# Attention and mixture-of-experts layers on one core: fused clips, rows transposed in place, ScalarE's order pinned, pieces of the schedule moved

## The chip, the cores and the metric

The kernel runs on one core of a Trainium2 chip. The metric is the device time of one execution in microseconds (us). A core has five engines that work side by side, each with a queue of its own: TensorE (PE in the profile; PEld is its loading of weights), VectorE (DVE), ScalarE (ACT), GpSimd (POOL) and SyncE (SP, which here only issues DMAs). All arithmetic is in f32.

## The reference, cut to what matters

Four layers run one after another over x of 8 sequences x 512 tokens x 256 features: attention a, experts, attention b, experts again with the same weights. Each layer adds to x a function of the normalised x.

```python
def attn_a(x):                       # 16 heads of 64
    q, k, v = split(x @ w_qkv)
    sim = (q * 64**-0.5) @ k.T + slopes * -abs(i - j)
    return softmax(where(j > i, -max, sim)) @ v @ w_out + b_out

def attn_b(x):                       # 8 heads of 128
    q, k = rope(x @ w_aq), rope(x @ w_ak)
    s = q @ k.T / 128 - 1e30 * (i < j)
    return softmax(s) @ (x @ w_av) @ w_ao

def ffn(x):                          # 8 experts, the best 2 of each token
    h = x * rsqrt(mean(x * x) + eps) * norm_w
    vals, idx = top_k(h @ gate_w.T + gate_b, 2)
    wts = softmax(vals)
    t1 = einsum('td,efd->tef', h, mlp1_w) + mlp1_b
    glu = minimum(t1[..., ::2], 7.0)
    lin = clip(t1[..., 1::2], -7.0, 7.0)
    act = glu * sigmoid(1.702 * glu) * (lin + 1.0)
    y = einsum('tei,edi->ted', act, mlp2_w) + mlp2_b
    return x + sum(y[idx] * wts)

x = x + attn_a(layernorm(x)); x = x + ffn(layernorm(x))
x = x + attn_b(layernorm(x)); x = x + ffn(layernorm(x))
```

## The kernel before

Tokens lie in tiles of 128 partitions, four to a sequence (`NT`). Only PE's order is that of the program; on the other engines the framework's scheduler orders instructions by its own estimate of when each is ready, except those that `keep_in_program_order` pins among each other.

**Attention.** `layer` steps through 8 sequences and 8 head groups. A step (`Attention.step`) puts on PE the scores of the current group, the transposes of the previous one (`turn`), the projections of the next and the weighted average of the previous. Scores get bias and row minimum on DVE (L387), exp on ACT (L397), and are divided by their sum on DVE and POOL (L412). Between these, `extra` runs pieces hung on a step: loading and normalising the next sequence, the output projection of the last one, and the first parts of the experts of the previous sequence.

**Choosing experts.** For each sequence `Experts.norm`, `apply`, `turn_norm`, `gates`, `choose` and `count` normalise x, store the rows h in DRAM, find each token's two experts and weights and count them. `choose` turns the gap of the two best logits into weights with an exp on ACT and three small DVE operations. For a group of sequences (six, then two: `GROUPS`), `sorting` then works out in pieces (`slots`, `pair`, `invert`, `tokens`) which token goes into which row of which block.

**Expert blocks.** `Experts.run` walks 55 + 23 blocks of 128 rows, each of one expert, as a software pipeline on PE: in turn n it issues `gather` for block n+4 (an indirect DMA on POOL, L867), `turn_act` for n-4 (transposes L927, ACT copy aT L929), `turn_rows` for n (transposes gtp L880, ACT copy hT L882), `first` for n-1 (matmuls hp L902, then on DVE and ACT the bias L912, clip L913, sigmoid L914, clip L916, products L917 and L918), and `second` for n-4 (matmuls y L937, bias L947, scatter of the rows to DRAM L948 on POOL). Then it runs the pieces hung on turn n, in `aside`.

Buffers limit how far this runs ahead: eight gathered rows (tag "qk", two tiles of `ROWS` = 4), four "S" tiles for the activations u, eight "kb" tiles that hold hT, aT and much else, and two "V" tiles for y.

**Pieces between blocks.** `flush` hangs on the first turns of an expert pass what attention left for the last sequence: the transposes and average of its last step, two pieces of output projection, then norm, apply, turn_norm, gates, choose and count; and after them the second group's sorting, three turns apart. From turn `done` (60), when the first group's rows are all written, the first pass fetches sequence 0 back for attention b and adds its expert rows; the second pass goes through six sequences by halves, fetching x, collecting rows (`collect`, L982) and adding (`add`, L1018), two turns apart, then stores the result (L1141). After the blocks the last two sequences are fetched, collected, added and stored.

## Time and profile before

| what | us |
|---|---|
| runs shown: median of 3 | 2336.51 |
| runs shown: lowest, highest | 2333.77, 2343.92 |
| profiled execution, its time | 2302.66 |
| its span, first to last instruction | 2300.8 |
| PE busy in the span | 2229.6 |

The stretches of the span are: attention a from the start to about 925 us, expert blocks to about 1196, attention b to about 2007, expert blocks to about 2276, then the last sums. In the profile's rows a name such as hp_f stands for the buffer written or read, `<-` parts output from inputs, `x` counts instructions. The bracket at the end of a row of the timeline is the engine's idle time before it and what ended it. A wait for several signals is put down to the one that came last. Idle time of an engine that is not the limit costs nothing. PE's instructions overlap, so two matmul rows can cover the same time.

### The profile page before, as it was taken

What the parts mean: (1) busy time and instruction counts of PE and PEld (TensorE: products, weight loads), DVE (VectorE), ACT (ScalarE), POOL (GpSimd) and SP (SyncE); (2) the same over time, 40 slices, a digit from 0 to 9 for tenths busy, and PEclk for the clock granted to TensorE, in tenths of its full rate; (3) what the DMA queues carried; (4) which work ended last, traced back from release to release, by engine and by line L of the source; (5) the groups of instructions that cost most, each with busy time, mean ns of one, the idle gap of its engine ahead of it and who ended that gap; (6) DMA issues with size and microseconds to landing.
All of it is one profiled execution on the core that took longest, in us unless ns stands there. A gap on an engine that the chain in (4) does not pass through costs nothing.

```text
span 2300.8 us, 34673 instructions
## 1 busy us (share of the span) xinstructions
PE 2229.6 (97%) x10657; PEld 1452.9 (63%) x10657; DVE 1635.5 (71%) x4926; ACT 977.9 (43%) x2828; POOL 989.9 (43%) x1374
## 2 busy tenths in 40 slices
PE   8999999999999999899999999999999999999994
PEld 5666666666666666556556666666666666665662
DVE  5566666666666777687877677776867678778787
ACT  4555555555555555323234343443433433433331
POOL 5443434343433343556644333343433434445662
PEclk9999999999999999999999999999999999999997
DMA  7100000000000001222310011010101000022247
GB/s 241 38 28 1 28 1 29 1 28 1 28 1 28 6 28 70 99 79 88 103 52 15 10 37 33 15 46 5 42 10 37 14 33 28 19 78 81 88 156 231
DMA packets 80005, 112.54 MB, mean 49 GB/s; under 512 B 10288, under 2 KB 64720, under 8 KB 79824
## 3 DMA queue, kind: packets, MB, share of 16 engines
q1 hardware_dynamic: 63760, 68.37, 9.0%
q0 software_dynamic: 14976, 40.91, 5.7%
q8 instruction: 89, 1.46, 0.3%
q10 hardware_dynamic: 1088, 1.05, 0.2%
q14 instruction: 92, 0.75, 0.1%
HBM read 68.86 MB, written 41.44 MB: 48 GB/s over the span
## 4 chain that ended last, share of the span: by engine, by line
PE 88%; DVE 7%; issue 2%; POOL 2%; ACT 1%; DMA 1%; DVEq 0%; ACTq 0%; POOLq 0%; SPq 0%
PE pp_a L317 9%; PE pp_b L317 9%; PE hp_f L902 9%; PE op_a L454 6%; PE sp_a L375 6%; PE tp_a L427 6%; PE sp_b L375 6%; PE op_b L454 5%; PE yp_b L472 5%; PE yp_a L472 5%; PE vp_a L298 5%; PE vp_b L298 5%; PE y_f L937 5%; PE tp_b L427 3%; PE atp_f L927 1%
## 5 line engine op out<-in xcount | busy, mean ns | idle before, releaser
L397 ACT ACTIVATE S_a<-S_a,nm_a 128x512 f32<-128x512 f32 (+3 forms) x512 | 280.3, 549 | 306.6 <-DVE nm_a L387 306.5
L330 POOL TENSOR_TENSOR qk_b<-qk_b,rot_b 128x512 f32<-128x512 f32 x128 | 162.8, 1272 | 457.0 <-DVE qk_b L329 446.8
L902 PE MATMUL hp_f<-we,hT_f 128*128 x624 | 294.4, 594 | 0.8 <-ACT hT_f L882 0.8
L356 POOL TENSOR_SCALAR ali_a<-alibi 128x512 f32<-128x512 f32 x128 | 79.4, 620 | 451.0 <-DVE nm_a L387 442.5
L397 ACT ACTIVATE S_b<-S_b,nm_b 128x512 f32<-128x512 f32 (+3 forms) x256 | 142.8, 558 | 235.3 <-DVE nm_b L387 233.8
L387 DVE CUSTOM_DVE_ANT_0 S_a<-sp_a,ali_a 128x512 f32<-128x512 f32 (+3 forms) x512 | 215.9, 486 | 30.7 <-PE sp_a L375 30.5
L412 POOL TENSOR_SCALAR S_a<-S_a,sum_a 128x384 f32<-128x384 f32 (+2 forms) x384 | 205.5, 551 | 34.7 <-DVE sum_a L408 26.2
L948 POOL DMA_INDIRECT y_f<-y_f,row_f x156 | 155.5, 997 | 131.6 <-DVE y_f L947 100.4
L867 POOL DMA_INDIRECT g_f<-h_all_f,token_f x156 | 152.1, 975 | 99.9 <-PE gtp_f L880 58.0
L914 ACT ACTIVATE u_f<-u_f 128x256 f32<-128x256 f32 x156 | 65.1, 417 | 305.0 <-DVE u_f L913 304.8
L937 PEld LDWEIGHTS y_f<-we,aT_f 128*128 128x128 f32 x624 | 117.2, 191 | 110.7 <-issue 53.3
L937 PE MATMUL y_f<-we,aT_f 128*128 x624 | 164.8, 387 | 21.6 <-ACT aT_f L929 21.6
L387 DVE CUSTOM_DVE_ANT_0 S_b<-sp_b,mask 128x512 f32<-128x512 f32 (+3 forms) x256 | 119.1, 484 | 90.5 <-PE sp_b L375 90.5
L375 PE MATMUL sp_b<-qk_b 128*128 128x512 f32 (+3 forms) x512 | 171.9, 438 | 5.0 <-POOL qk_b L330 5.0
L427 PE MATMUL tp_a<-ident,S_a 128*128 128x128 f32 x1280 | 165.3, 276 | 1.1 <-DVE O_a L462 0.6
L427 PEld LDWEIGHTS tp_a<-ident,S_a 128*128 128x128 f32 x1280 | 141.1, 141 | 31.9 <-issue 22.8
L454 PE MATMUL op_a<-PT_a,V_a 128*64 128x384 f32 (+3 forms) x1024 | 154.2, 439 | 3.3 <-ACT PT_a L437 2.2
L912 DVE TENSOR_TENSOR u_f<-hp_f,be 128x512 f32<-128x512 f32 x156 | 107.8, 691 | 68.8 <-PE hp_f L902 61.0
L375 PE MATMUL sp_a<-qk_a 64*128 64x512 f32 (+3 forms) x1024 | 155.5, 443 | 0.9 <-DVE qk_a L334 0.9
L902 PEld LDWEIGHTS hp_f<-we,hT_f 128*128 128x128 f32 x624 | 106.8, 191 | 76.0 <-issue 74.8
L437 ACT COPY PT_a<-tp_a 128x512 f32<-128x512 f32 (+1 forms) x320 | 138.6, 495 | 29.4 <-PE tp_a L427 29.4
L454 PE MATMUL op_b<-PT_b,V_b 128*128 128x512 f32 (+3 forms) x512 | 148.6, 433 | 0.0
(184 smaller groups left out, 4505.6 us busy)
## 6 DMA issues: line engine op xcount, KB each, us to landing
h_all_f<-hn_f SPq DMA_DIRECT2D x64, 128.0 KB, 1.7
xm_f<-x_mid_f SPq DMA_DIRECT2D x16, 512.0 KB, 4.1
yg_f<-y_f SPq DMA_DIRECT2D x64, 128.0 KB, 2.2
yg_f<-y_f SPq DMA_DIRECT2D x28, 256.0 KB, 4.0
x<-x_in_dram SPq DMA_DIRECT2D x8, 512.0 KB, 4.1
we<-w_dram SPq DMA_DIRECT2D x8, 512.0 KB, 7.1
x_mid_f<-x SPq DMA_DIRECT2D x8, 512.0 KB, 2.9
x_mid_f<-xm_f SPq DMA_DIRECT2D x8, 512.0 KB, 3.0
```

The lines of the kernel that those rows point to most:

```text
L298: nc.tensor.matmul(vp[:, k, :], lhsT=self.xT[b][:, c, t * P : (t + 1) * P], rhs=wv[:, c, q * 2 * P : (q + 1) * 2 * P], start=(c == 0), sto ...
L317: nc.tensor.matmul(pp, lhsT=w[:, c, g * P : (g + 1) * P], rhs=self.xT[b][:, c, :], start=(c == 0), stop=(c == NC - 1),)
L330: nc.gpsimd.tensor_tensor(qk[:, j, :], qk[:, j, :], rot, ALU.add)
L375: nc.tensor.matmul(sp[i][:, at[it] : at[it] + w], lhsT=qk[r, 0, it * P : (it + 1) * P], rhs=qk[r, 1, 0:w], start=True, stop=True,)
L387: nc.vector.tensor_tensor_reduce(out=s, in0=sp[i][:, at[it] : at[it] + w], in1=add[i][:, T - w : T], scale=scale, scalar=float(np.finfo(np ...
L397: nc.scalar.activation(s, s, AF.Exp, bias=nm[:, it : it + 1], scale=-1.0, accum_out=sums[:, it : it + 1],)
L412: eng.tensor_scalar(s, s, sums[:, it : it + 1], 1.0, ALU.mult, ALU.mult)
L427: nc.tensor.transpose(tp[:, o : o + P], S[:, S_OFF[it] + jt * P : S_OFF[it] + (jt + 1) * P], ident,)
L454: nc.tensor.matmul(op[i * cols : (i + 1) * cols, jt * P : T], lhsT=v[:, jt, c0 : c0 + cols], rhs=PT[i][:, P_OFF[jt] : P_OFF[jt] + T - jt * P],
L472: nc.tensor.matmul(yp[:, 0:D], lhsT=o[:, c, t * P : (t + 1) * P], rhs=wo[:, half * HALF + c, :], start=(c == 0), stop=(c == HALF - 1),)
L902: nc.tensor.matmul(hp, lhsT=h[:, c * P : (c + 1) * P], rhs=we_sb[:, bass.DynSlice(wat + c * 2 * FI, 2 * FI)], start=(c == 0), stop=(c == N ...
L937: nc.tensor.matmul(yp, lhsT=aT[:, c * P : (c + 1) * P], rhs=we_sb[:, bass.DynSlice(wat + NC * 2 * FI + c * D, D)], start=(c == 0), stop=(c ...
```

## The change

- **Clips.** The minimum of the gate half, L913, goes. The sigmoid reads the unclipped value; the product with the other half clips it on the way, and the product with the sigmoid clips that at sigmoid(1.702 x 7). Output g has a place of its own.
- **In place.** hT is written over the gathered rows, aT over the first half of t.
- **ScalarE's order.** The copies hT and aT and the sigmoid are pinned.
- **Start.** The first sequence comes in four transfers on two queues, and PE does 24 transposes of the identity that nothing reads.
- **Choose.** In the last sequence of a pass both weights are sigmoids of the gap and of its negative.
- **Pieces.** `flush` hangs its pieces on other turns, the sorting four turns apart. In the second pass x comes back in pairs into attention's weight buffers at turns 24 to 42; halves are collected 1.5 turns apart into two tags by turns, added four turns later, and stored by one DMA. The last two sequences have no fetch of their own, and their stores alternate between SP's and ACT's queue.

```diff
+S_LIMIT = float(1.0 / (1.0 + np.exp(-ALPHA * LIMIT)))
...
-    X = {0: load_x(x_in[0], "x0")}
+    X = {0: xpool.tile([P, NT, D], F32, tag="x", name="x0")}
+    for t in range(NT):
+        (nc.sync, nc.scalar)[t % 2].dma_start(
+            out=X[0][:, t, :], in_=x_in[0][t * P : (t + 1) * P, :]
+        )
...
     make_identity(nc, ident)
+    idle = ps.tile([P, P], F32, tag="ps", bufs=8, name="idle")
+    for _ in range(24):
+        nc.tensor.transpose(idle, ident, ident)
...
+            if among_blocks:
+                for k in range(2):
+                    nc.scalar.activation(
+                        r["w"][k][:, here], gap, AF.Sigmoid, scale=(1.0, -1.0)[k]
+                    )
+            else:
...
-            h = work.tile([P, D], F32, tag="kb", bufs=8, name=f"hT_{key}")
-            nc.scalar.copy(h, tp)
+            h = g
+            made = nc.scalar.copy(h, tp)
+            tc.keep_in_program_order(made)
...
-            t, g, a = u[:, 0 : 2 * FI], u[:, 2 * FI : 3 * FI], u[:, 3 * FI : 4 * FI]
-            s = u[:, 4 * FI : 5 * FI]
+            t, s = u[:, 0 : 2 * FI], u[:, 2 * FI : 3 * FI]
+            g, a = u[:, 3 * FI : 4 * FI], u[:, 4 * FI : 5 * FI]
+            lin = t[:, FI : 2 * FI]
             nc.vector.tensor_tensor(t, hp, be_sb[:, bass.DynSlice(bat, 2 * FI)], ALU.add)
-            nc.vector.tensor_scalar(g, t[:, 0:FI], LIMIT, 1.0, ALU.min, ALU.mult)
-            nc.scalar.activation(s, g, AF.Sigmoid, scale=ALPHA)
-            lin = t[:, FI : 2 * FI]
+            made = nc.scalar.activation(s, t[:, 0:FI], AF.Sigmoid, scale=ALPHA)
+            tc.keep_in_program_order(made)
             nc.vector.tensor_scalar(lin, lin, 1.0 - LIMIT, 1.0 + LIMIT, ALU.max, ALU.min)
-            nc.vector.tensor_tensor(g, g, lin, ALU.mult)
-            nc.vector.tensor_tensor(a, g, s, ALU.mult)
-            self.act[i, j] = a, wat, bat
+            nc.vector.scalar_tensor_tensor(g, t[:, 0:FI], LIMIT, lin, ALU.min, ALU.mult)
+            nc.vector.scalar_tensor_tensor(a, s, S_LIMIT, g, ALU.min, ALU.mult)
+            self.act[i, j] = a, t[:, 0:FI], wat, bat
...
-            aT = work.tile([P, FI], F32, tag="kb", bufs=8, name=f"aT_{key}")
-            nc.scalar.copy(aT, tp)
+            made = nc.scalar.copy(aT, tp)
+            tc.keep_in_program_order(made)
...
+        def fetch_pair(self, b, tag):
+            pair = wpool.tile([P, 2, NT, D], F32, tag=tag, name=f"xm_{self.kind}_{b}")
+            for k in range(2):
+                X[b + k] = pair[:, k]
+                nc.sync.dma_start(out=pair[:, k], in_=by_tokens(self.x_mid[b + k]))
...
-        turns = (1, 2, 3, 4, 4, 5, 7, 8, 9, 11)
+        turns = (-3, 0, 1, 1, 1, 3, 6, 8, 10, 12)
...
-            aside[14 + 3 * n] = [piece]
+            aside[16 + 4 * n] = [piece]
...
-    n = done
-    for b in range(*GROUPS[0]):
-        aside.setdefault(n, []).append(lambda b=b: exp_b.fetch(b))
-        for tt in ((0, 1), (2, 3)):
-            aside.setdefault(n, []).append(
-                lambda b=b, tt=tt: exp_b.collect(b, tt, "PT", both_queues)
-            )
-            aside.setdefault(n + 3, []).append(lambda b=b, tt=tt: finish(b, tt))
-            n += 2
+    for k, tag in enumerate(("wq", "wk", "wv", "wo")):
+        aside.setdefault(24 + 6 * k, []).append(lambda k=k, tag=tag: exp_b.fetch_pair(2 * k, tag))
+    halves = [(b, tt) for b in range(*GROUPS[0]) for tt in ((0, 1), (2, 3))]
+    for k, (b, tt) in enumerate(halves):
+        n = done + 3 * k // 2
+        tag = ("xT", "PT")[k % 2]
+        aside.setdefault(n, []).append(
+            lambda b=b, tt=tt, tag=tag: exp_b.collect(b, tt, tag, both_queues)
+        )
+        aside.setdefault(n + 4, []).append(lambda b=b, tt=tt: finish(b, tt, nc.sync))
...
-    for b in range(*GROUPS[1]):
-        exp_b.fetch(b)
-        for tt in ((0, 1), (2, 3)):
-            exp_b.collect(b, tt, "S", (nc.sync, nc.scalar))
-    for b in range(*GROUPS[1]):
-        for tt in ((0, 1), (2, 3)):
-            finish(b, tt)
+    last = [(b, tt) for b in range(*GROUPS[1]) for tt in ((0, 1), (2, 3))]
+    for b, tt in last:
+        exp_b.collect(b, tt, "S", (nc.sync, nc.scalar))
+    for k, (b, tt) in enumerate(last):
+        finish(b, tt, (nc.sync, nc.scalar)[k % 2])
```

More of the change, by code (lines that the diff above doesn't have):

```diff
@@ L631, in gates, with choose @@
             self.h[b] = lgT
-        def choose(self, b):
+        def choose(self, b, among_blocks=False):
             kind = self.kind
@@ L670, in choose @@
             nc.vector.tensor_tensor(gap, top[0], top[1], ALU.subtract)
-            fall = t2("fall")
-            nc.scalar.activation(fall, gap, AF.Exp, scale=-1.0)
-            nc.vector.tensor_scalar_add(gap, fall, 1.0)
-            nc.vector.reciprocal(r["w"][0][:, here], gap)
-            nc.vector.tensor_tensor(r["w"][1][:, here], r["w"][0][:, here], fall, ALU.mult)
+            if among_blocks:
[4 more added lines that the diff above has]
+            else:
+                fall = t2("fall")
+                nc.scalar.activation(fall, gap, AF.Exp, scale=-1.0)
+                nc.vector.tensor_scalar_add(gap, fall, 1.0)
+                nc.vector.reciprocal(r["w"][0][:, here], gap)
+                nc.vector.tensor_tensor(r["w"][1][:, here], r["w"][0][:, here], fall, ALU.mult)
             self.both[b] = t3("both")
@@ L909, in first @@
             u = work.tile([P, PACKED], F32, tag="S", bufs=4, name=f"u_{key}")
-            t, g, a = u[:, 0 : 2 * FI], u[:, 2 * FI : 3 * FI], u[:, 3 * FI : 4 * FI]
-            s = u[:, 4 * FI : 5 * FI]
+            t, s = u[:, 0 : 2 * FI], u[:, 2 * FI : 3 * FI]
+            g, a = u[:, 3 * FI : 4 * FI], u[:, 4 * FI : 5 * FI]
+            lin = t[:, FI : 2 * FI]
             nc.vector.tensor_tensor(t, hp, be_sb[:, bass.DynSlice(bat, 2 * FI)], ALU.add)
-            nc.vector.tensor_scalar(g, t[:, 0:FI], LIMIT, 1.0, ALU.min, ALU.mult)
-            nc.scalar.activation(s, g, AF.Sigmoid, scale=ALPHA)
-            lin = t[:, FI : 2 * FI]
+            made = nc.scalar.activation(s, t[:, 0:FI], AF.Sigmoid, scale=ALPHA)
+            tc.keep_in_program_order(made)
             nc.vector.tensor_scalar(lin, lin, 1.0 - LIMIT, 1.0 + LIMIT, ALU.max, ALU.min)
-            nc.vector.tensor_tensor(g, g, lin, ALU.mult)
-            nc.vector.tensor_tensor(a, g, s, ALU.mult)
-            self.act[i, j] = a, wat, bat
+            nc.vector.scalar_tensor_tensor(g, t[:, 0:FI], LIMIT, lin, ALU.min, ALU.mult)
+            nc.vector.scalar_tensor_tensor(a, s, S_LIMIT, g, ALU.min, ALU.mult)
+            self.act[i, j] = a, t[:, 0:FI], wat, bat
         def turn_act(self, i, j):
             key = f"{self.kind}_{i}_{j}"
-            a, wat, bat = self.act.pop((i, j))
+            a, aT, wat, bat = self.act.pop((i, j))
             tp = ps.tile([P, FI], F32, tag="ps", bufs=8, name=f"atp_{key}")
@@ L998, in collect @@
             m = (b - GROUPS[i][0]) * NT + tiles[0]
-            bufs = {"S": 4, "PT": 2, "tmp": 3}[tag]
+            bufs = {"S": 4, "xT": 2, "PT": 2, "tmp": 3}[tag]
             got = work.tile(
@@ L1063, in layer @@
             put(b + 1, 4, 1, lambda b=b: exp.gates(b))
-            put(b + 1, 5, 1, lambda b=b: exp.choose(b))
+            put(b + 1, 5, 1, lambda b=b: exp.choose(b, b + 1 == NB))
             put(b + 1, 6, 1, lambda b=b: exp.count(b))
@@ L1117, in layers @@
     aside = flush(layer(att_a, exp_a, more), exp_a)
-    aside[6] = [weights_b]
+    aside.setdefault(6, []).append(weights_b)
     aside[done] = [lambda: exp_a.fetch(0)]
@@ L1136, in layers, with finish @@
     aside = flush(layer(att_b, exp_b, more), exp_b)
-    def finish(b, tiles):
+    def finish(b, tiles, engine):
         exp_b.add(b, tiles)
-        for t in tiles:
-            nc.sync.dma_start(out=by_tokens(out[b])[:, t, :], in_=X[b][:, t, :])
-    n = done
-    for b in range(*GROUPS[0]):
-        aside.setdefault(n, []).append(lambda b=b: exp_b.fetch(b))
-        for tt in ((0, 1), (2, 3)):
-            aside.setdefault(n, []).append(
-                lambda b=b, tt=tt: exp_b.collect(b, tt, "PT", both_queues)
-            )
-            aside.setdefault(n + 3, []).append(lambda b=b, tt=tt: finish(b, tt))
-            n += 2
+        engine.dma_start(
+            out=by_tokens(out[b])[:, tiles[0] : tiles[-1] + 1, :],
+            in_=X[b][:, tiles[0] : tiles[-1] + 1, :],
+        )
[7 more added lines that the diff above has]
+            lambda b=b, tt=tt, tag=tag: exp_b.collect(b, tt, tag, both_queues)
+        )
+        aside.setdefault(n + 4, []).append(lambda b=b, tt=tt: finish(b, tt, nc.sync))
     end = sum(BLOCKS) + 4
     exp_b.run(aside)
-    for m in range(end, n + 3):
+    for m in range(end, n + 5):
         for piece in aside.get(m, ()):
             piece()
-    for b in range(*GROUPS[1]):
-        exp_b.fetch(b)
-        for tt in ((0, 1), (2, 3)):
-            exp_b.collect(b, tt, "S", (nc.sync, nc.scalar))
-    for b in range(*GROUPS[1]):
-        for tt in ((0, 1), (2, 3)):
-            finish(b, tt)
+    last = [(b, tt) for b in range(*GROUPS[1]) for tt in ((0, 1), (2, 3))]
[3 more added lines that the diff above has]
+        finish(b, tt, (nc.sync, nc.scalar)[k % 2])
 def _tables():
```

## The prediction

> **What bounds the kernel now.** First the page: busy shares, then the span in 40 slices.
>
> ```profile
> PE 2229.6 (97%) x10657; PEld 1452.9 (63%) x10657; DVE 1635.5 (71%) x4926; ACT 977.9 (43%) x2828; POOL 989.9 (43%) x1374
> PE   8999999999999999899999999999999999999994
> ```
>
> TensorE is the bound; no edit removes a needed matmul, so all there is to win is the 71.2 us (2300.8 - 2229.6) in which it idles, and the stretches where it ran slowly. Busy time by stretch (stretch, length, PE, PEld, DVE, ACT, POOL, clock, DMA) places them:
>
> ```profile
> 0.00:58.00 58.00, 47.89 (x233) 29.38 (x233) 29.64 (x115) 28.09 (x85) 33.95 (x68) 1.00 0.70 239
> 900.00:1000.00 100.00, 91.30 (x463) 58.64 (x460) 74.48 (x258) 38.10 (x106) 48.79 (x60) 1.00 0.33 111
> 1000.00:1100.00 100.00, 100.00 (x406) 63.13 (x405) 81.54 (x215) 31.90 (x101) 64.04 (x66) 1.00 0.27 86
> 2275.00:2301.00 26.00, 0.65 (x4) 0.22 (x2) 13.79 (x31) 0.00 (x0) 1.99 (x2) 0.55 0.79 262
> ```
>
> Steady expert blocks run at 100%, one per 3.02 us. Idle are the start (10.1), the opening of each expert pass, its close, and the tail (25.4). The waits (total, times, longest) name the releaser:
>
> ```profile
> PE y_f L937 <- ACT aT_f L929: 21.6, 25, 2.4
> PE xtp_a L255 <- DVE xn_a L242: 8.6, 1, 8.6
> PE tp_b L427 <- POOL S_b L412: 2.5, 1, 2.5
> ```
>
> ACT is named for 21.6 us, but in the timeline it was itself held by DVE:
>
> ```profile
> 956.65 0.28 DVE L913 TENSOR_SCALAR u_f<-u_f 128x256 f32<-128x256 f32 x1
> 956.96 0.42 ACT L914 ACTIVATE u_f<-u_f 128x256 f32<-128x256 f32 x1 [5.65 <-DVE u_f L913]
> 957.28 0.35 ACT L929 COPY aT_f<-atp_f 128x256 f32<-128x256 f32 x1
> 957.69 1.13 PE L937 MATMUL y_f<-we,aT_f 128*128 x4 [2.45 <-ACT aT_f L929]
> 970.90 1.28 ACT L914 ACT_TABLE_LOAD   x1
> 972.92 1.13 PE L937 MATMUL y_f<-we,aT_f 128*128 x4 [1.19 <-ACT aT_f L929]
> ```
>
> The copy aT needs only PE's transposes, but stands in ACT's queue behind a later block's sigmoid, whose input waits for a burst of DVE work. The chain that ended last gives both ends:
>
> ```profile
> 0.73 4.22 DMA x<-x_in_dram
> 8.65 1.77 PE xtp_a L255 x7
> 11.18 5.41 PE pp_a L317 x8
> 23.52 1.72 PE pp_a L317 x4
> 2276.83 6.01 DMA y_f<-y_f,row_f
> 2285.95 5.70 DMA yg_f<-y_f
> ```
>
> Eight pp_a matmuls took 5.41 us where four later take 1.72: 3.44 at full clock.
>
> **The sum**, stage by stage, in the profiled execution's own time.
>
> **Start.** x0's statistics start at 4.97 when 512 KB has landed and end at 6.74. In four transfers the first three tiles' statistics (about 0.45 each) lie under the landing. 128 KB transfers elsewhere land in 1.7 to 2.2 us; here all four share the engines with wq, so I put the last at 4.7 (3.9 to 5.5), the end at 5.3: **1.4** saved (0.6 to 2.2). wq and wk are issued one DMA (0.44) later and land at about 7.9 and 10.5, needed at about 9.2 and 11.0. The two issues on ACT's queue come before its first 1.28 us table load, otherwise half the gain goes. The 24 transposes cost PE only idle time: at the slow 0.22 us each, 5.3 us from the identity's end at 1.47, so until 6.8, and xn arrives at about 7.1. Here row and rule differ. By the row half speed lasted 6.05 us, 8.65 to 14.70, so the warm clock would come at about 7.5. The Trainium skill (TensorE: Matmul & The Clock Gate, Part 1) wants one busy window of about 3.4 us, on a grid that runs free of the kernel: an estimate from it is clock up between 4.9 and 8.3. Row: pp_a falls from 5.41 to 3.44 and the transposes by 0.5, **2.5** saved. Rule at its late end: 0.5 less. The page's granted clock shows 1.00 here and doesn't decide it. I take the row; bounds 0 to 2.5. Start: **3.9** (0.6 to 4.7).
>
> **The block's own work.** DVE drops L913 (0.28; 0.21 net of overlap). The two fused products keep the tensor products' price: a fused one with a pointer scalar costs 480 ns (L1018) against 425 (L918), but with an immediate 0.19 both (L667, L663, 128x32); at worst 0.11 per block. L917 no longer overwrites what the sigmoid reads, a wait of 0.25 to 0.34 where DVE is behind. So 0.21 per block where PE covers it (worth nothing, 3.02 stays), about 0.45 where DVE is the limit. hT over g and aT over t remove no instruction. They hold buffers longer: u until L937, which precedes the next user's matmul on PE anyway; g's rows until hp instead of gtp, so every fourth gather waits about 4.7 us longer (y 0.86, the transposes 0.44, two hp 3.44). Scatters and POOL norms stand behind it. It still issues 10 us before its transposes, and gather plus landing is 1.0 + 2.8: hidden, 6 us to spare. The pinned ACT order (aT, hT, sigmoid) is the order the steady trace shows already: 0.
>
> **Opening of pass one.** L937's waits are 2.45 (norm applied), 1.19 (choose), 0.35 + 0.77 + 1.46 (slots, pairs). Choosing by sigmoid removes the last sequence's two table loads. By the row, 1.28 each with PE waiting 1.19; by the skill (ScalarE: Activation LUTs, What ACT_TABLE_LOAD costs) about 2.66 a switch, so 5.3 per pass. No second half is seen after the load: the sigmoid starts at 972.20, 1.30 after 970.90. I take 1.0. Norm to apply is now two short blocks (3.9) instead of one of 3.02, so DVE stands less behind POOL's rsqrt chain (1.86 there): 2.45 to 1.5, bounds 0 to 3. Sorting four blocks apart instead of three, with 0.21 freed in each: 2.58 to 1.1. Sum **3.4** (0 to 6). The moved last turn and average carry 20 transposes and their ACT/DVE copies; S_a is ready by 926.6, so 0. On SP, apply's four row stores and its x_mid store go two turns earlier; only weights_b stands behind them, needed 60 blocks later.
>
> **Close of pass one.** DVE-bound blocks of 4.06, 3.76, 4.10 and 3.89 us instead of 3.02, and one wait of 1.83. Four blocks at 0.45 and 1.2 off the wait (two sigmoids no longer stand behind L913, which took 0.80 and 0.86 there): **3.0**. Around 1192 to 1200 the clock fell to half after sparse work (about 3.1 lost); a third of that back: **1.0**. Bounds 1 to 7.5.
>
> **Opening of pass two.** The same 3.4, and half of a clock dip at 2042 to 2046 (1.7): 0.8. Against it: the last turn now stands ahead of every block, but S_b L412 sits behind eight gathers in POOL's queue until 2013.3. Gathers 0 and 1's transposes and hp(0), 2.5 us that filled this hole, come after: PE waits about 5.4 instead of 2.5. Net **1.7** (-3 to 9; the top if POOL serves S_b first).
>
> **Close of pass two and tail.** Twelve half-sequence sums (4 adds of 0.44) now come every 1.5 blocks: 1.17 us of DVE per block, not 0.88. With the rest of the block at 2.05 to 2.3 that is 3.2 to 3.45 against 3.02. Over 17 blocks 3.4 to 7.3, of which the pipeline absorbed 1.7 before; I put the stall at 2.5 and 0.5 in the drain. Before, 3.6 in blocks and 1.8 in the drain: **2.4**. The eight x fetches go earlier on SP (0.37 each, ahead of the collects; 4 MB in all, at blocks 24 to 42, when SP has nothing else), and the last out writes leave the tail (one DMA of 256 KB for two of 128; the final four alternate with ACT's queue, where nothing stands behind them), so the last scatter, 6.01 in traffic of 290 GB/s, lands in 3.5 (typical 2.5): **2.5**. From 2282.8 the before needs 17.9 us: about 4 MB at 330 GB/s, with the last reads held on SP to 2287.9 behind a fetch. After: first half at 4.0, four times 1.88 of adds, then 3.5 from last add to end as before: 15. **2.9**. Together **7.8** (2 to 13).
>
> Sum: 3.9 + 3.4 + 4.0 + 1.7 + 7.8 = **20.8 us**. The profiled execution took 2302.66 (span 2300.8 and 1.86 around it), so about 2282. The runs shown have a median of 2336.51, 33.85 above it, for which the profile gives no cause; I take the same difference off: **2315.7**.
>
> **Rivals.** (a) The waits only move: DVE's bursts are as long, and pinned ACT holds aT behind the sigmoid as before. For it: the 2.45 wait is just that order, unchanged. Openings give 1.0 each from table loads less 2.5, closes 2, start 3.9, tail 5.4: 10.8 saved, **2325.7**. (b) Everything recovers: both clock dips gone, S_b first on POOL, no stall at 1.5 blocks: start 4.7, 6 + 6, 6, 11: 33.7, **2302.8**. Against it: DVE's 3.2 per block. (c) Slower: gathers held until hp become late, PE waits at gtp. Price: x us for each of 39 groups of four rows. It cancels the gain at 0.53, and from 0.84 the kernel is over 0.5% slower; at 1.0, **2354.7**. Against it: POOL is busy 64 of 100 us and the 6 us to spare.
>
> **Numbers.** Main case 0.50, (a) 0.26, (b) 0.16, (c) 0.08. About 0.5% (11.7 us) is what this measurement can tell from nothing. Main and (b) are faster, (a) straddles 2324.8 evenly: faster 0.79, same 0.13, slower 0.08. The range runs from just under (b), 2300, to 2331, where (a) with its runs' spread of some 5 us ends; outside lie (c) and the edges.
>
> **What would show it.** pp_a's first eight at 3.5 us and sp_a starting near 13.6; one ACT_TABLE_LOAD per pass; L937's waits near 10 in total; tp_b's wait 5 if POOL keeps its order; DVE over 95% in the last 17 blocks; last scatter landing under 4 us and 15 us after it. It is wrong if PE waits at gtp_f on g_f, if half clock returns before xtp_a, or if L937's waits stay near 20.

## The result and the profile after

| | us |
|---|---|
| before, 8 runs: median (lowest to highest) | 2342.24 (2333.77 to 2344.70) |
| changed, 8 runs: median (lowest to highest) | 2325.02 (2317.98 to 2332.04) |
| changed / before | 0.9939, 95% interval 0.9918 to 0.9959 |
| profiled execution of the changed kernel, its span | 2324.46, 2322.7 |

The change makes the kernel about 0.6% faster. One thing has to be known for what follows: the profiled execution of before that the prediction was read from took 2302.66 us, 31 us less than any of its eight timed runs, so the two given profiles can't be subtracted from each other. The first experiment, b_again, deals with that.

The page of the changed kernel: busy time of the engines, and PE's busy tenths in 40 slices.

```profile
PE 2244.4 (97%) x10681; PEld 1454.0 (63%) x10681; DVE 1597.2 (69%) x4764; ACT 976.3 (42%) x2826; POOL 997.2 (43%) x1374
PE   8999999999999999999999999999999999999995
```

DVE has 162 instructions fewer, PE the 24 idle transposes more. The stretches of the changed kernel, with the columns of before (length, busy PE, PEld, DVE, ACT, POOL, granted clock, DMA share, GB/s):

```profile
0.00:58.00 58.00, 49.97 (x239) 30.38 (x240) 28.30 (x104) 24.64 (x71) 32.66 (x65) 0.97 0.71 239
900.00:1000.00 100.00, 92.86 (x456) 58.87 (x455) 67.39 (x230) 35.11 (x102) 46.49 (x56) 0.98 0.32 105
1000.00:1100.00 100.00, 95.58 (x390) 59.02 (x389) 70.82 (x180) 30.34 (x93) 62.23 (x62) 1.00 0.26 82
2297.00:2323.00 26.00, 4.74 (x22) 3.14 (x20) 15.20 (x37) 1.42 (x4) 4.53 (x5) 0.68 0.52 176
```

From 1000 to 1100 us PE did 406 matmuls in the profile of before and does 390 here: the steady blocks, which the prediction took as fixed at 3.02 us, are slower in this profile. Its waits (total, times, longest):

```profile
PE y_f L956 <- ACT u_f L947: 28.2, 31, 3.0
PE tp_b L437 <- POOL S_b L422: 5.4, 1, 5.4
PE y_f L956 <- issue: 5.2, 9, 1.2
PE tp_a L437 <- DVE O_a L472: 3.3, 2, 2.6
PE xtp_a L265 <- DVE xn_a L252: 0.9, 1, 0.9
```

The wait of xtp_a went from 8.6 to 0.9 because the idle transposes now fill that time. The waits of y are 28.2 us, not the forecast 10; what they have to be compared with comes under b_again. A new wait of 2.6 on O_a has come. At the end, the chain that ended last:

```profile
2305.45 2.81 DMA y_f<-y_f,row_f
2308.44 4.00 DMA yg_f<-y_f
```

The last scatter lands in 2.81 us instead of 6.01. From its landing (2308.26) to the end of the span are 14.4 us; it was 17.9.

### The profile page after: what moved, and what is told of

It reads as the page before. It is cut to its first block, busy times and chain, and to the rows that moved or that the text cites. A ratio compares the mean times of both kernels' runs of the same rounds, so it can differ in the third digit from the quotient of the medians.

```text
span 2322.7 us, 34444 instructions
## 1 busy us (share of the span) xinstructions
PE 2244.4 (97%) x10681; PEld 1454.0 (63%) x10681; DVE 1597.2 (69%) x4764; ACT 976.3 (42%) x2826; POOL 997.2 (43%) x1374
## 4 chain that ended last, share of the span: by engine, by line
PE 85%; DVE 7%; issue 2%; DMA 2%; ACT 1%; POOL 1%; another core or an unknown queue 1%; DVEq 0%; SPq 0%; ACTq 0%; POOLq 0%
PE pp_b L327 9%; PE pp_a L327 9%; PE hp_f L921 8%; PE op_a L464 6%; PE sp_a L385 6%; PE tp_a L437 6%; PE sp_b L385 6%; PE y_f L956 5%; PE op_b L464 5%; PE yp_b L482 5%; PE yp_a L482 5%; PE vp_a L308 4%; PE vp_b L308 4%; PE tp_b L437 3%; PE gtp_f L897 1%
## 5 line engine op out<-in xcount | busy, mean ns | idle before, releaser
L921 PE MATMUL hp_f<-we,g_f 128*128 x624 | 295.7, 596 | 1.0 <-issue 1.0
L956 PE MATMUL y_f<-we,u_f 128*128 x624 | 166.6, 390 | 34.6 <-ACT u_f L947 28.2
L956 PEld LDWEIGHTS y_f<-we,u_f 128*128 128x128 f32 x624 | 114.4, 190 | 132.7 <-ACT u_f L947 64.3
L884 POOL DMA_INDIRECT g_f<-h_all_f,token_f x156 | 156.8, 1005 | 69.6 <-issue 67.9
L437 PEld LDWEIGHTS tp_a<-ident,S_a 128*128 128x128 f32 x1280 | 141.1, 141 | 35.9 <-issue 21.4
L921 PEld LDWEIGHTS hp_f<-we,g_f 128*128 128x128 f32 x624 | 107.2, 192 | 77.0 <-issue 76.9
```

The source lines that it names most:

```text
L437: nc.tensor.transpose(tp[:, o : o + P], S[:, S_OFF[it] + jt * P : S_OFF[it] + (jt + 1) * P], ident,)
L921: nc.tensor.matmul(hp, lhsT=h[:, c * P : (c + 1) * P], rhs=we_sb[:, bass.DynSlice(wat + c * 2 * FI, 2 * FI)], start=(c == 0), stop=(c == N ...
L956: nc.tensor.matmul(yp, lhsT=aT[:, c * P : (c + 1) * P], rhs=we_sb[:, bass.DynSlice(wat + NC * 2 * FI + c * D, D)], start=(c == 0), stop=(c ...
```

## The experiments

The kernels below ran on four chips, called A to D. The kernel before took 2347.1, 2304.1, 2339.7 and 2338.0 us on them (medians of 11 to 22 runs), so what is compared is each kernel's ratio to the kernel before on the same chip, and across chips with care. To place a difference I took marks out of each trace: the last score matmul of an attention layer, and the end of the y matmuls of blocks 0, 20, 60 and 77 (counted from 0) of each expert pass. Where experts' blocks are late by a few us in one profile and not in the next, a mark moves by 3 to 5 us; single marks closer than that are not read.

**b_again** is the kernel before with no edit, profiled a second time (chip A).

> The kernel before, unchanged, profiled again. Theory A (the profiled execution of 2302.66 us was an unusual one, the stretched blocks in the profile after come with most executions of either kernel): a time of 2334 to 2345 us, PE busy 92 to 97 us of the 100 between 1000 and 1100 us instead of 100.00, and blocks of 3.3 to 5.4 us among those of 3.02; attention a and b as long as in the first profile within 3 us each. Rival B (the changed kernel alone stretches its blocks): again 100.00 of 100 and 3.02 us per block, and the time above 2302 lies elsewhere, in the attention stretches.

Measured: 2344.07 us. Attention a takes 900.8 us from its first score to its last, the same as in the first profile. Expert pass one takes 300.5 us from the last score of attention a to its last y, instead of 278.6; pass two 289.7 instead of 270.3. That is the whole difference. The stretch of steady blocks, in b_again:

```profile
1000.00:1100.00 100.00, 92.41 (x372) 56.41 (x372) 72.87 (x198) 29.01 (x89) 57.29 (x59) 1.00 0.25 78
```

A part of its timeline shows what a slow block looks like:

```profile
1084.57 1.03 PE L937 MATMUL y_f<-we,aT_f 128*128 x4
1085.66 0.38 PE L880 MATMUL gtp_f<-ident,g_f 128*128 128x128 f32 x2
1087.34 0.37 ACT L882 COPY hT_f<-gtp_f 128x256 f32<-128x256 f32 x1 [3.18 <-PE gtp_f L880]
1087.35 0.69 DVE L912 TENSOR_TENSOR u_f<-hp_f,be 128x512 f32<-128x512 f32 x1 [3.14 <-PE gtp_f L880]
1087.76 1.56 PE L902 MATMUL hp_f<-we,hT_f 128*128 x3 [1.72 <-ACT hT_f L882]
```

By its rows PE was done with the hp that L912 reads at 1084.7 and with gtp at 1086.0. But L912 and the copy both start at 1087.35, within 0.01 us of each other: PE's semaphore, which both wait for, stood still for 3 us, and then took five increments within 0.21 us. I counted such bursts in the semaphore events (no increment for 1.5 us although matmuls that increment were done, then four within 0.35 us). In every profile of chips A, C and D and in the given one of the changed kernel there are some 10 to 20 of them, all in the expert passes, the longest 5.5 us late. On chip B no profile has one, nor has the first profile of before. Theory A holds: the first profile was the unusual one, and the bursts are no work of the change. That they make up the whole difference fits in sum (in b_again the delays add up to about 42 us, and it is 41 us longer), but not stretch by stretch: blocks 20 to 60 of pass one in old_start, below, lose 11.5 us with a single such burst of 2.8 us. So part of the lost time is not explained.

For the waits of y, b_again is the profile to compare with:

```profile
PE y_f L937 <- ACT aT_f L929: 36.3, 35, 2.4
```

Beside bursts they went from 36.3 us to 28.2 in the changed kernel, and to 21.3 in a second profile of it.

**fixed**: is it the register that PE and DVE load with each block's expert? Each block gets a fixed expert; PE's and DVE's loads of it fall away, and the rows are computed with other experts' weights.

```diff
-            wat = self.at_block(i, j, 0, mybir.EngineType.PE, W_COLS)
-            bat = self.at_block(i, j, 1, mybir.EngineType.DVE, B_COLS)
+            wat = (j % NE) * W_COLS
+            bat = (j % NE) * B_COLS
```

> The kernel before with the expert of each block fixed in the program (block j uses expert j mod 8), so that PE and VectorE load no register from memory; the expert rows are then computed with other experts' weights. Theory A (PE's signals come late, in bursts, because of these register loads): no bursts, blocks of 3.02 us, each expert pass about 268 us from its last score matmul instead of 290 to 300, ratio 0.983. Rival B (the bursts go with the indirect transfers of rows, which only the expert passes have, or with something else of them): bursts of 2 to 5 us as in the other profiles, ratio 0.996 or more.

Measured on chip B: 2302.58 us, ratio 0.9993 (0.9985 to 1.0002). As chip B has no bursts even in the other kernels, this run says only that the loads cost nothing there in sum (its block 20 comes 5.4 and 3.7 us later than in the first profile of before, its blocks 60 to 77 take 2.6 and 4.6 less). What makes the bursts stays open.

**old_start** and **x1_pin** (chip A) take the start apart. old_start is the changed kernel with the old start:

```diff
-    X = {0: xpool.tile([P, NT, D], F32, tag="x", name="x0")}
-    for t in range(NT):
-        (nc.sync, nc.scalar)[t % 2].dma_start(
-            out=X[0][:, t, :], in_=x_in[0][t * P : (t + 1) * P, :]
-        )
+    X = {0: load_x(x_in[0], "x0")}
...
-    for _ in range(24):
-        nc.tensor.transpose(idle, ident, ident)
```

> The changed kernel without the four transfers of x0 and without the 24 idle transposes. Theory A (DVE's queue got another order: the statistics of sequence 1 stand ahead of the copy of O_a and wait 5.0 us for their transfer): the start itself is 2.7 us slower (sp_a at 17.4), the statistics come behind the copy again, the clock doesn't fall at 42 us, and the second average's start at 49 us instead of 52.5: 3.5 us less than with the change, ratio to before about 0.9925. Rival B (the prediction): 3.9 us more than with the change, ratio 0.9955.

x1_pin keeps the new start and pins two kinds of instruction on DVE:

```diff
-            nc.vector.bn_stats(out=st[:, t, :], in_=X[b][:, t, :])
+            made = nc.vector.bn_stats(out=st[:, t, :], in_=X[b][:, t, :])
+            if (key, b) == ("a", 1):
+                tc.keep_in_program_order(made)
...
-                nc.vector.tensor_copy(self.O[b][:, g % HALF, :], op)
+                made = nc.vector.tensor_copy(self.O[b][:, g % HALF, :], op)
+                if b == 0:
+                    tc.keep_in_program_order(made)
```

> The changed kernel, with the copies of O_a of sequence 0 and the statistics of sequence 1 pinned in the program's order on DVE, so that the statistics come four steps later. Theory A (the order alone costs 5.2 us): sp_a still at 14.8, no wait of tp_a on O_a, the second average at 47.3, 5.2 us less than with the change through the rest of attention a; ratio about 0.9917. Rival B (another wait takes its place, such as xn of sequence 1 becoming late): the second average at 47.3 too, but the offset is back to 3.5 us by the first step of sequence 1; ratio 0.9939.

Measured: old_start 2333.30 us, ratio 0.9942 (0.9929 to 0.9956); x1_pin 2329.18 us, 0.9923 (0.9909 to 0.9937). Start of the averages of the first two steps of attention a:

| | average 1 | average 2 | later steps, up to the last but one |
|---|---|---|---|
| before, first profile | 35.0 | 49.1 | (taken as the measure) |
| old_start | 35.9 | 50.0 | the same distance |
| changed (two profiles) | 33.3, 34.4 | 52.5, 51.7 | the same distance |
| x1_pin | 33.4 | 49.1 | the same distance |
| turns_b (below; same start and pins) | 33.4 | 47.5 | the same distance |

DVE in the kernel before has the copy of O_a first:

```profile
37.61 0.69 DVE L462 COPY O_a<-op_a 128x512 f32<-128x512 f32 x1 [1.78 <-PE op_a L454]
38.22 0.41 DVE L233 BATCH_NORM_STATS2 st_a<-x 128x6 f32<-128x256 f32 x1
```

The timeline of the changed kernel between these two marks:

```profile
39.06 0.75 DVE L243 BATCH_NORM_STATS2 st_a<-x 128x6 f32<-128x256 f32 x2 [4.96 <-DMA x<-x_in_dram]
40.74 0.66 DVE L472 COPY O_a<-op_a 128x512 f32<-128x512 f32 x1
41.45 1.05 PE L437 MATMUL tp_a<-ident,S_a 128*128 128x128 f32 x6 [2.64 <-DVE O_a L472]
42.67 3.28 PE L327 MATMUL pp_a<-xT_a,wq_a 128*128 128x512 f32 x4 [0.17 <-DVE nm_a L397]
```

and of x1_pin:

```profile
35.86 0.69 DVE L474 COPY O_a<-op_a 128x512 f32<-128x512 f32 x1 [1.62 <-PE op_a L466]
39.51 1.66 PE L439 MATMUL tp_a<-ident,S_a 128*128 128x128 f32 x10 [1.34 <-POOL S_a L424]
41.01 1.88 PE L329 MATMUL pp_a<-xT_a,wq_a 128*128 128x512 f32 x4
```

With the earlier start the scheduler puts the statistics of sequence 1 ahead of the copy of O_a on DVE (in before and in old_start they come after it). They wait 4.96 us for a transfer that doesn't come earlier, and PE waits behind the copy. In this profile PE then falls to half speed, and four matmuls take 3.28 us instead of 1.88; in the second profile of the change (wait 2.0 us) they take 1.98. Between the two averages the change takes 19.2 and 17.3 us instead of 14.1, x1_pin 15.7, and turns_b, with the same start and the same pins, 14.1 again: its second average starts at 47.5 us, where theory A of x1_pin had 47.3. So theory A holds for the cause and, in turns_b, for the size. x1_pin still lost 1.6 us at a wait on POOL's division of S_a, after POOL itself had waited three times for expert weights to land (0.48, 0.48 and 0.72 us); that much is what rival B said of another wait, but it did not come in turns_b.

The last score of attention a ends between 918.2 and 919.6 us in all nine profiles with the old start (mean 918.9), at 921.8 and 921.0 in the change and 923.4 in no_pins (below), which has the same start. The start as made therefore loses 2 to 4.5 us there. Repaired, it gains 0.4 (x1_pin) and about 2 (turns_b).

The timed runs don't show this: old_start's interval holds rival B's 0.9955 and not theory A's 0.9925, and its ratio is that of the change (0.9939) within the noise. The expert passes stand in between: in old_start they took 294.2 and 291.9 us, in the change 285.5 and 290.5, on another chip. I go by the marks, since this stage repeats so closely. The medians of old_start and x1_pin, both of chip A, lie 4.1 us apart, which the profiles don't show; but the profiled execution of x1_pin was its slowest, 2334.22 us, and the intervals overlap.

**block_only**, **end_only** and **open_only**: each a part of the change alone on the kernel before. block_only (chip A) has the clips, hT and aT in place and the pins, as in the change's diff.

```diff
-            nc.vector.tensor_scalar(g, t[:, 0:FI], LIMIT, 1.0, ALU.min, ALU.mult)
...
-            nc.vector.tensor_tensor(g, g, lin, ALU.mult)
-            nc.vector.tensor_tensor(a, g, s, ALU.mult)
+            nc.vector.scalar_tensor_tensor(g, t[:, 0:FI], LIMIT, lin, ALU.min, ALU.mult)
+            nc.vector.scalar_tensor_tensor(a, s, S_LIMIT, g, ALU.min, ALU.mult)
```

> The kernel before with only the edits inside the expert block: fused clips, rows transposed in place, ScalarE's copies and sigmoid pinned. Theory A (PE covers DVE in the steady blocks; only the DVE-bound blocks at the closes gain 0.45 us each): 3 to 5 us less than before, ratio 0.998 to 0.9985. Rival B (in most executions many blocks are not covered, and 0.21 us of DVE counts in each of 78): 16 us, ratio 0.993, which would be nearly the whole gain. Rival C (the pins or the longer held buffers cost): ratio above 1.000, with waits of aT or gtp that the profile before doesn't have.

Measured: 2346.02 us, ratio 0.9999 (0.9989 to 1.0009). Nothing, so the 4 us of A did not come either. The nothing is a sum, though. Against b_again on the same chip the waits of y grew from 36.3 to 45.7 us and block 20 comes 3.7 and 3.6 us later in the two passes, while the part after the last y takes 22.0 us instead of 25.3:

```profile
PE y_f L940 <- ACT u_f L931: 45.7, 39, 3.5
```

These are single profiles; that a loss in the openings hides a gain elsewhere is possible and not shown.

end_only (chip B) has the reads in pairs, the halves 1.5 turns apart, one store per half:

```diff
+    for k, tag in enumerate(("wq", "wk", "wv", "wo")):
+        aside.setdefault(24 + 6 * k, []).append(lambda k=k, tag=tag: exp_b.fetch_pair(2 * k, tag))
+    halves = [(b, tt) for b in range(*GROUPS[0]) for tt in ((0, 1), (2, 3))]
+    for k, (b, tt) in enumerate(halves):
+        n = done + 3 * k // 2
```

> The kernel before with only the new end: x fetched back in pairs at blocks 24 to 42, halves summed every 1.5 blocks, one store for each half. Theory A (the prediction: 7.8 us, of which 2.5 is the last scatter, 2.9 the tail and 2.4 the blocks): from the last y matmul to the end 18 us instead of 25, ratio 0.9965 to 0.997. Rival B (the sums every 1.5 blocks stretch the last blocks, since the fetched halves collide with DVE's block work): the tail gains 7 us too, but the second expert pass gets 3 us or more longer, ratio 0.9985.

Measured: 2298.49 us, ratio 0.9973 (0.9964 to 0.9983). From the last y to the end 18.3 us instead of 25.1 to 25.6, and pass two 270.9 us, where before has 270.3: theory A for the tail, no gain in the blocks and no loss.

open_only (chip B) has the turns, the sorting and the sigmoids of `choose`:

```diff
-        turns = (1, 2, 3, 4, 4, 5, 7, 8, 9, 11)
+        turns = (-3, 0, 1, 1, 1, 3, 6, 8, 10, 12)
...
-            aside[14 + 3 * n] = [piece]
+            aside[16 + 4 * n] = [piece]
```

> The kernel before with only the new opening: the weights of the last sequence by sigmoid, the pieces on other turns, the sorting four turns apart. Theory A (what is left of the gain once the end has its 7 us and the block edits nothing): 6 us of pass one, from its last score matmul to its last y 294 instead of 300.5 us, nothing in pass two, where the wait of tp_b on S_b takes it; ratio 0.9970 to 0.9978. Rival B (the prediction's sum for both openings, 5.1 us, split 3.4 and 1.7): ratio 0.9978, with pass two shorter as well. Rival C (the openings gain only beside the lighter blocks): ratio 0.999 or more.

Measured: 2313.25 us, ratio 1.0042 (1.0028 to 1.0056): slower. Theory A and rival B fall; it lies in the range of rival C (0.999 or more), which gave no reason for a loss. PE in the opening of pass one:

```profile
943.20 1.88 PE L909 MATMUL hp_f<-we,hT_f 128*128 x4
945.35 1.88 PE L909 MATMUL hp_f<-we,hT_f 128*128 x4
951.79 0.80 PE L944 MATMUL y_f<-we,aT_f 128*128 x1 [4.55 <-ACT aT_f L936]
```

and ACT:

```profile
951.06 0.42 ACT L921 ACTIVATE u_f<-u_f 128x256 f32<-128x256 f32 x1 [3.70 <-DVE u_f L920]
951.38 0.35 ACT L936 COPY aT_f<-atp_f 128x256 f32<-128x256 f32 x1
```

The first block's aT stands behind a sigmoid that waits 3.70 us for DVE. In ACT's queue three sigmoids of later blocks are ahead of it there; for all other blocks of this kernel, and for all blocks of the change with its pins, it is two at most. The same happens in pass two (4.5 us), and both times PE runs at half speed after it (by the profile's clock from 950.2 to 957.0 and from 2042.5 to 2045.9 us). That suggested that the pins make the opening pay.

**open_pins** (chip C) is open_only with ACT's order pinned; **no_pins** (chip D) is the change without the pins; **open_place** (chip D) is open_pins with hT and aT in place, clips still as before; **after_again** (chip C) is the change itself.

```diff
-            nc.scalar.copy(aT, tp)
+            made = nc.scalar.copy(aT, tp)
+            tc.keep_in_program_order(made)
```

> The kernel before with the new opening and ScalarE's order pinned (copies hT and aT, sigmoid), without fused clips and in-place rows. Theory A (open_only lost since ScalarE's queue had the first block's aT behind the third sigmoid in each pass, 4.6 and 4.5 us of waiting and a fall of the clock after it; pinned, it stands behind the second as everywhere): no wait of y over 3 us in the openings, no half clock at 930 to 960, 10 to 14 us less than open_only, ratio 0.997 to 0.999 where the kernel before takes 2304 us, and below 0.997 where it takes 2345. Rival B (what cost was the transposes ahead of all blocks, and the lighter blocks made up for it in the change): the waits shrink but the time stays within 4 us of open_only, ratio 1.002 to 1.004.

> The changed kernel without the three pins on ScalarE; 14 of the 156 copies aT then stand one sigmoid earlier in its queue, all others as with the pins. Theory A (the prediction: the pins are worth nothing): the ratio of the change, 0.9936, within 0.0015. Rival B (the pins cost, since copies that could go ahead of a waiting sigmoid are held): 3 to 6 us less in the first twenty blocks of the passes, ratio 0.991. Rival C (the pins are what makes the new opening pay): 5 us or more longer, ratio 0.996 or more.

```diff
-            h = work.tile([P, D], F32, tag="kb", bufs=8, name=f"hT_{key}")
+            h = g
...
-            aT = work.tile([P, FI], F32, tag="kb", bufs=8, name=f"aT_{key}")
```

> The kernel before with the new opening, ScalarE's order pinned, and hT and aT in place; the clips as before. Theory A (the new opening crowds DVE's norm and sorting into the first twenty blocks, and the instruction and the wait that the fused clips take out of each block are what makes it pay): as slow as open_pins, ratio 1.006 to 1.009 where the kernel before takes 2340 us. Rival B (hT and aT stood in the ring of eight small tiles beside the norm's rows, which the new turns hold longer, and moving them out of it makes it pay): ratio 0.996 to 0.998, the 20th block of each pass 5 to 8 us earlier than in open_pins.

> The changed kernel, unchanged, once more. Theory A (where the kernel before takes 2304 us, PE's signals come in time, and the parts add up as measured so far: what turns_b has at 2285.0, plus 5.2 us for the wait on sequence 1 and 2.9 us for the wait on S_b): 2293 us, ratio 0.9953; where the kernel before takes 2345 us, 2331 us, ratio 0.994. Rival B (the wait on sequence 1 and the wait on S_b don't count there): 2285 us where the kernel before takes 2304.

| new opening with | chip | ratio to before | interval | block 20 ends at, pass one, pass two |
|---|---|---|---|---|
| the pins (open_pins) | C | 1.0085 | 1.0066 to 1.0103 | 112.1, 111.1 |
| the pins, in place (open_place) | D | 1.0052 | 1.0037 to 1.0066 | 106.6, 104.3 |
| all block edits, new end (old_start) | A | 0.9942 | 0.9929 to 0.9956 | 106.0, 104.7 |
| the whole change (after_again) | C | 0.9936 | 0.9922 to 0.9949 | 101.3, 102.4 |
| the change without pins (no_pins) | D | 0.9931 | 0.9917 to 0.9945 | 103.8, 100.1 |
| for comparison: before (b_again) | A | 1 | | 107.9, 100.0 |

(The marks count from the last score of the attention layer before the pass.)

The idea of the pins fell. open_pins has no wait of y over 2.5 us before 1000 us, but it is the slowest kernel of all, slower than either of its theories had it, and the change without the pins is as fast as with them. How much of the loss is the pins' is not told apart, since open_only ran on the chip without bursts and open_pins has the most of them. Rows in place seem to help the opening: block 20 comes 5.5 and 6.8 us earlier than in open_pins, as rival B of open_place said, but the ratio fell by 0.0033 where B gave 0.0105 to 0.0125, and 1.0052 is close to theory A. The rest of the way, from 1.0052 to 0.9942 less the 0.0027 of the end, I put down to the fused clips: by ratios 0.8%, by the two profiles 11 us in the two passes. That is a subtraction across chips, with the end's part taken from chip B; no kernel had the new opening and the fused clips alone, so the size is uncertain.

after_again took 2323.30 us. Its two theories part only where the kernel before takes 2304 us, so it doesn't decide between them.

**turns_b** (chip B) is x1_pin with the last step's transposes in pass two back behind the first block:

```diff
-    aside = flush(layer(att_b, exp_b, more), exp_b)
+    aside = flush(layer(att_b, exp_b, more), exp_b, (1, 2, 3, 3, 3, 5, 7, 9, 11, 13))
```

> The changed kernel with the pinned statistics of sequence 1, and in the second expert pass the last step's transposes and average on turns 1 and 2 as before (the rest on 3, 3, 3, 5, 7, 9, 11, 13). Theory A (the transposes ahead of every block cost PE the 5.4 us in which POOL works through eight gathers): the wait of tp_b back to 2.5, 2 to 3 us less than with x1_pin in pass two, ratio 0.991. Rival B (the first blocks only trade places, and norm, choose and the second sorting come one turn later): the same time as x1_pin, ratio 0.9923, with longer waits of y at the later pieces.

Measured: 2285.03 us, ratio 0.9918 (0.9905 to 0.9932). tp_b waits 2.6 us, and block 20 of pass two ends at 93.2 us where before has 97.5 on a profile without bursts; in the change it comes at 102.7 and 102.4 where b_again has 100.0. That supports theory A; the ratio doesn't, as its interval holds A's 0.991 and rival B's 0.9923. The waits of y are the shortest of all profiles, where the first profile of before, also without bursts, has 21.6:

```profile
PE y_f L960 <- ACT u_f L951: 12.8, 19, 1.8
```

The kernel is 19 us faster than before on chip B; the change itself was not run there and turns_b not on the other chips, so that it beats the change is likely, not measured. Its steady blocks:

```profile
1000.00:1100.00 100.00, 100.00 (x408) 63.41 (x407) 73.54 (x186) 31.47 (x100) 65.94 (x66) 1.00 0.29 85
```

## Why the prediction was right, and where its steps were wrong

The forecast was 2315.7 us with 20.8 us gained; measured were 2325.02 and 17.2 between the medians. Sign, size and range hold. The absolute time is 9.3 us off, and 5.7 of these lie in the median of before, which was 2336.51 over three runs and is 2342.24 over eight. Stage by stage the sum held much less well than its total: that the total fits is luck in good part. The table sets b_again beside two profiles of the change with bursts (the given one, and after_again); negative is a gain. The chips differ, and before is slower on that of b_again (2347.1 us, against 2339.7 where after_again ran), so the sum of 20.1 is larger than the timed gain of 16 to 17 us, and the stages of the expert passes are the ones that can't be trusted to a few us.

| stage | forecast | b_again | changed, two profiles | difference |
|---|---|---|---|---|
| start to first score | -3.9 | 18.6 | 14.8, 16.8 | -2.8 |
| first to last score of attention a | 0 | 900.8 | 907.0, 904.1 | +4.8 |
| pass one to block 20 | -3.4 | 107.9 | 100.3, 101.3 | -7.1 |
| blocks 20 to 60 | 0 | 136.4 | 129.6, 131.7 | -5.8 |
| blocks 60 to 77 | -4.0 | 56.2 | 55.6, 55.5 | -0.6 |
| attention b, last y to last score | 0 | 807.3 | 806.7, 806.7 | -0.6 |
| pass two to block 20 | -1.7 | 100.0 | 102.7, 102.4 | +2.5 |
| blocks 20 to 60 | 0 | 135.7 | 133.8, 131.3 | -3.2 |
| blocks 60 to 77 | -2.4 | 53.9 | 54.0, 53.7 | 0.0 |
| last y to the end | -5.4 | 25.3 | 18.2, 17.8 | -7.3 |
| sum | -20.8 | | | -20.1 |

The start with attention a, the closes of the two passes and the opening of pass two came out about 16 us worse than forecast; the opening of pass one, the forty blocks that were put at nothing, and the tail came out about 15 us better.

**Start: the mechanism right in part, the gain gone a little later.** The changed kernel's first instructions:

```profile
1.52 4.84 PE L172 MATMUL idle<-ident 128*128 128x128 f32 x24 [1.52 <-POOL ident masks.py:199]
7.22 1.41 PE L265 MATMUL xtp_a<-ident,xn_a 128*128 128x128 f32 x8 [0.86 <-DVE xn_a L252]
9.31 1.98 PE L327 MATMUL pp_a<-xT_a,wq_a 128*128 128x512 f32 x4 [0.68 <-DVE xT_a L296]
11.90 1.98 PE L327 MATMUL pp_a<-xT_a,wk_a 128*128 128x512 f32 x4 [0.61 <-DMA wk_a<-a_qkv_dram]
14.76 1.45 PE L385 MATMUL sp_a<-qk_a 64*128 64x512 f32 x6 [0.88 <-DVE qk_a L344]
```

The 24 transposes begin 0.21 us apart, at half speed (forecast 0.22). In this profile the last five begin about 0.11 apart, so the clock came up among them, at 5.7 us by the profile's record of the clock; x1_pin and turns_b agree (5.7 and 5.5). In after_again and no_pins all 24 are slow, and it came up only about when the real transposes began (7.3 and 6.9 by the profile's clock). The shortest transpose shows it (ns, lowest, median, highest), in the given profile and in after_again:

```profile
L172 PE MATMUL idle<-ident x24: 272/421/473, 1.5 to 6.1; 128*128 128x128 f32 x24
L172 PE MATMUL idle<-ident x24: 421/421/473, 1.5 to 6.5; 128*128 128x128 f32 x24
```

So the row that I took (6.05 us of half speed, up at 7.5) was later than all five profiles with the new start, and the estimate from the Trainium skill's page (TensorE: Matmul & The Clock Gate, Part 1: 4.9 to 8.3) holds all five; that the moment changes from one profile of the same program to the next agrees with a grid that runs free of the kernel. The row was one draw: half speed lasts 6.0 us in the first profile of before and 8.3 in b_again. The latter is more than the 6.8 us that the same estimate gives at most; PE paused in between there, for 0.6 us, and whether that is the reason is not shown.

What the sum missed at once: wk lands at 11.9 instead of 10.5 and is waited for; in after_again it is wq, for 2.0 us, and PE falls back to half speed:

```profile
10.60 3.62 PE L327 MATMUL pp_a<-xT_a,wq_a 128*128 128x512 f32 x4 [1.97 <-DMA wq_a<-a_qkv_dram]
```

The first eight pp_a then take 5.6 us, as long as before (5.41), where the given profile has 4.0 and the forecast 3.5. What it missed further on: the step "sp_a starts at 13.6" was taken for the end of the stage. An earlier start changes the scheduler's order on DVE, and the second sequence's transfer had no reason to be earlier. This step failed: by the marks it cost 2 us or more instead of gaining 3.9.

**The block's own work: "worth nothing where PE covers" was right on one chip only, and wrong for the openings.** Without bursts, blocks 20 to 60 take 120.8 to 121.3 us in every kernel of chip B and in the first profile of before, 3.02 each, whatever DVE does, and blocks 60 to 77 of pass one fall from 58.0 to 54.4 (turns_b), near the 3.0 plus 1.0 of the sum. With bursts, the cover is gone: the forty blocks took 132.5 to 139.2 us with the old clips (three profiles, two passes each, mean 136.3) and 129.6 to 136.9 with the fused ones (six profiles, mean 132.5). So a lighter DVE may be worth some 4 us a pass there, perhaps because DVE has to catch up after each burst. It is not shown: the bursts scatter as much as that, and block_only, which differs from b_again in the block alone and ran on the same chip, took 4.0 us less in one pass and 1.2 more in the other. I had the 33.85 us between the profile and the runs in my hand, called them without a cause, and took them off as a constant. They were no constant: nearly all of them lay in the stage whose cover my zeros rested on.

**In place and pins.** "Hidden, remove no instruction" missed the ring of eight small tiles: hT and aT stood there beside the four norm rows of a sequence, which the new turns hold from turn 3 to turn 6. That this ring is the cause is argued; the runs show only that with them out of it block 20 comes 6 us earlier beside the new opening, on another chip. For the pins the forecast of 0 is right (0.9931 against 0.9936).

**Openings: right in total, wrong as a part.** The sum counted 5.1 us for the new turns, nearly all of it by themselves. Alone they cost 9.1 us on chip B; with pins, 20 us on chip C; only beside the lighter block do they gain, and in pass one alone. The sum added edits that share a resource, DVE's and ACT's time in the first twenty blocks, as if each were alone. The table loads did go as forecast: one per pass, 1.28 us each; the second half that the Trainium skill (ScalarE: Activation LUTs, What ACT_TABLE_LOAD costs) would add, 2.66 us a switch in all, is in no row, so the row was the right one to take. In pass two the loss was named and sized to a tenth: POOL's queue holds S_b behind eight gathers. PE in the kernel before, then PE and POOL in the changed kernel there:

```profile
2012.92 1.65 PE L427 MATMUL tp_b<-ident,S_b 128*128 128x128 f32 x10 [2.48 <-POOL S_b L412]
```

```profile
2021.61 2.63 PE L437 MATMUL tp_b<-ident,S_b 128*128 128x128 f32 x10 [5.40 <-POOL S_b L422]
2024.46 3.27 PE L464 MATMUL op_b<-PT_b,V_b 128*128 128x512 f32 x8
```

```profile
2017.15 0.94 POOL L884 DMA_INDIRECT g_f<-h_all_f,token_f  x1 [0.30 <-issue]
2018.39 0.94 POOL L884 DMA_INDIRECT g_f<-h_all_f,token_f  x1 [0.30 <-issue]
2019.64 0.94 POOL L884 DMA_INDIRECT g_f<-h_all_f,token_f  x1 [0.30 <-issue]
2020.62 1.39 POOL L422 TENSOR_SCALAR S_b<-S_b,sum_b 128x384 f32<-128x384 f32 x3
```

What was left out is the clock after that hole, at half from 2019.5 to 2026.4 us by the profile's clock: the ten transposes take 2.63 us where before has 1.65, eight of op_b 3.27 where the others take 2.32. By the table the opening of pass two loses 2.5 us where the sum gave 1.7 gained.

**Close of pass two and tail.** The tail term was too small (5.4 against 7.3), the block term (2.4) came to nothing. DVE is busy 43.4 of the 47 us from 2250 to 2297, 92%, not over 95. That the halves 1.5 turns apart fill what the fused clips set free would be an easy account, but the runs don't bear it out: end_only, with the old clips, took 52.7 us for these blocks (DVE 97%), turns_b, with the fused ones, 55.1 (91%), before 52.1 (93%). What sets the time there stays open.

By its own sign ("wrong if L937's waits stay near 20") the prediction would have failed, with 28.2 and 21.3 us. But that number was read from a profile without bursts. Like beside like, the waits fell from 36.3 us, and without bursts from 21.6 to 12.8 in turns_b, whose start and second pass are repaired.

Of the rivals, (a) gave 2325.7, which is nearest to the 2325.02 measured. Its account was another: the waits did shrink, the start doesn't hold and the forty blocks gain. (b) needed S_b first on POOL, and POOL kept its order; the clock dip at the close of pass one is gone, but in b_again it is gone too, and pass two has dips from 2019.5 and 2070.7 us. (c) is refuted: no wait of gtp on g in any profile.

## What to carry to other kernels

Before a stage's cost is put at nothing because another engine covers it, look whether the profiled execution is like the timed runs; if it is 30 us off, find the stage in which it differs, for a cover that holds in the one may be open in the other. Edits that meet in one stage are not summed but run together and apart: here one part alone cost 0.4%, with pins 0.9%, another alone gave nothing, and both together gained. And where a scheduler orders by its own estimates, a start that comes sooner reorders what follows: follow it until the next transfer that doesn't come sooner.

## What the runs showed of the hardware

On three of four chips PE's completions reached the other engines late, in bursts: some 10 to 20 times per execution, up to 5.5 us late, four increments then within 0.35 us, and only in the expert passes, though the page gives a granted clock of 1.00 there and PE's own rows, whose ends are modelled, go on until they need what DVE or ACT was to deliver. On the fourth chip there was none, and the same kernel took 2304 instead of 2338 to 2347 us. Attention took the same on all of them (900.3 to 901.0 us with the old start).

The late blocks don't fall at random. Over 3.4 us took, of blocks 21 to 60 in pass one, 22, 25, 26, 30, 33, 34, 38, 42, 46, 50 and 56 in b_again, and 23, 28, 31, 36, 39, 44, 47, 52, 55 and 58 in old_start; pass two has nearly the same. So something that recurs in the program every few blocks seems to set their place, while it went with the chip whether they came at all. The register loads of the blocks, their indirect transfers and the loading of instructions (89 packets of 16 KB in nearly every profile, with bursts or without) were not told apart as the cause.
